# A four-layer kernel: the last layer's polar network cut into 64 pieces and dealt out between the waves of its attention

## The chip, the cores and the metric

The kernel runs on one core of a Trainium2 chip. The core has five engines with a queue of instructions each: TensorE (PE; matrix products, written to the eight banks of PSUM), VectorE (DVE), ScalarE (ACT; functions, from tables that are loaded in sets), GpSimd (POOL) and SyncE (SP, which here only issues transfers). Each engine takes its instructions in order; an instruction waits on semaphores for what others make. The metric is the device time of one execution in microseconds (us). Three runs of the kernel before took 4312.2, 4317.82 and 4314.3 us: a median of 4314.3 us.

## The reference, cut to what matters

The input x has 2 batches of 2048 tokens of width 256. Each of four layers normalises x and adds an attention-like part and a feed-forward part to it. The first three layers (gated linear attention and a mixture of experts; a state-space block and product-key experts; an exponential average with a dense block and a network of binary weights) are the same before and after. The change lies in layer 3:

```python
def _L3_attn_ref(x, q_proj_weight, k_proj_weight, v_proj_weight, o_proj_weight):
    # 16 heads of 16
    q, k, v = (split_heads(x @ w.T) for w in (q_proj_weight, k_proj_weight, v_proj_weight))
    scores = jnp.einsum('bhtc,bhkc->bhtk', q, k) * 16 ** (-0.5)
    scores = jnp.where(causal, scores, -jnp.inf)
    attn = jax.nn.softmax(scores, axis=-1)
    out = jnp.einsum('bhtk,bhkc->bhtc', attn, v)
    return merge_heads(out) @ o_proj_weight.T

def _L3_ffn_ref(x, theta, phi, theta_noise, phi_noise):
    real = jnp.einsum('bti,io->bto', x, jnp.cos(theta + theta_noise))
    imag = jnp.einsum('bti,io->bto', x, jnp.sin(phi + phi_noise))
    return jnp.sqrt(real * real + imag * imag)

xn = _layernorm(x, axis=-1)
x = x + _L3_attn_ref(xn, ...) + _L3_ffn_ref(xn, ...)
```

The second function is called the polar layer here. All arithmetic is in 32-bit floats.

## The kernel before

x stays in SBUF as 32 tiles of 128 tokens by 256 (`g.x`), 16 per batch. Its normalised transpose, `g.xT`, has two blocks of 128 features by 4096 tokens.

**Layer 2's end.** `layer2` runs eight blocks of 512 tokens. The binary network of one block goes beside the dense block of the next, and so the last block's binary network runs alone: PE makes products, ACT and DVE split each into two parts (lines 1009 and 1010, tile `hb`), DVE adds the sum to x (line 1043).

**The polar layer of batch 0.** `four_layers` then opens a pool and calls `layer3_ffn`. It makes the 256 by 512 matrix of cosines and sines, `cs`, in `polar_weights`: eleven DVE operations bring the angles into range, and two ACT operations take the sine. Four times it normalises four tiles (`norm`, line 71), transposes them on PE (`turn`, line 87), multiplies each tile with `cs` (512 columns, two halves of the contraction), squares, sums, takes the root and adds to x. These instructions are placed by the scheduler of the framework.

**The attention.** All of `layer3_attn` from line 1479 on is inside `tc.manual_schedule()`: there the order of each engine's instructions is the order in which the code writes them. Its work goes by eight groups of four heads (two batches by four groups). For a group, `qk` makes queries and keys in eight pieces of 256 tokens: two ACT copies out of PSUM, and four transfers by SP that bring each head's 16 key rows to a partition that is a multiple of 32 (line 1192). `waves` walks over 40 units of a causal score matrix, of 128 by up to 512, with four heads each:

- for one group (`gm`) the scores with queries on the partitions (tile `ps_m`, line 1365), whose row maxima DVE takes (line 1386); `fold` brings the maxima into the query tile of that group;
- for the group before (`ge`), whose maxima are known, the scores with keys on the partitions (tile `ps_e`, line 1361), whose exponential ACT takes into `pt` (line 1375), POOL masks the diagonal (line 1379), and PE multiplies with the values (line 1416, tile `ps_v`). `divide` divides by the sums, `prod` multiplies with the output weights.

A matrix of 32 rows takes a quarter of PE's rows, so four of these scores run side by side. First there is a stage with maxima alone, for group 0; it is called solo here. Seven stages do `ge` and `gm` together: a unit is then two waves, each with two heads of the one and two heads of the other, in the order e, m, e, m. The last stage has `ge` alone.

Between the waves small pieces of work are dealt out: `fill` (one after a unit in the paired stages, at an even pace in the solo stage), `pieces` on PE that have come due through `later`, and `steps` on other engines. In the paired stages a piece borrows one of the four banks of `ps_m`; the exponent scores have three banks. In the solo stage the fill is batch 1's polar layer (`polar`, line 1427: norms on ACT and DVE, transposes, 16 products), the 16 value projections of batch 0 and the eight `qk` pieces of group 1. The values lie in `vals`, 256 columns per token tile; `spread` (line 1209) copies a group's 64 columns on POOL into one of two tiles `vv`, 32 columns per head with a one in the 17th, so that the sum of the probabilities comes out as a 17th row. The value projections of batch 1 are due during the stage of groups 2 and 3.

Of the kernel before, what the change touches and what calls it, by code (L numbers as in the profile page):

```python
# [14 lines left out]
F32 = mybir.dt.float32  # L15
# [1034 lines left out]
def polar_weights(g, pool, a, cs):  # L1050


    nc = g.nc
    th = pool.tile([P, 4, 512], F32, name="th")
    nc.sync.dma_start(th, a["l3_th"])
    an = pool.tile([P, 2, 512], F32, name="an")
    n = pool.tile([P, 2, 512], F32, name="an_n")
    nc.vector.tensor_tensor(an[:, 0, :], th[:, 0, :], th[:, 1, :], ALU.add)
    nc.vector.tensor_tensor(an[:, 1, :], th[:, 2, :], th[:, 3, :], ALU.add)
    nc.vector.tensor_scalar(n[:, 0, :], an[:, 0, :], 0.15915494309189535, 0.25, ALU.mult, ALU.add)  # L1060
    nc.vector.tensor_scalar(n[:, 1, :], an[:, 1, :], 0.15915494309189535, None, ALU.mult)
    nc.vector.tensor_scalar(n, n, 12582912.0, None, ALU.add)
    nc.vector.tensor_scalar(n, n, 12582912.0, None, ALU.subtract)
    for c in (6.28125, 0.0019350051879882812, 3.019916050561733e-07):
        nc.vector.scalar_tensor_tensor(an, n, -c, an, ALU.mult, ALU.add)
    nc.vector.tensor_scalar(an[:, 0, :], an[:, 0, :], 1.5707963267948966, None, ALU.add)
    nc.vector.tensor_scalar(an, an, 3.1415925, -3.1415925, ALU.min, ALU.max)
    for w in range(2):
        nc.scalar.activation(cs[:, :, w * D : (w + 1) * D], an[:, w, :].rearrange("p (k n) -> p k n", k=2), AF.Sin)


def layer3_ffn(g, tc, a):

    nc = g.nc
    F = g.polar
    wk = F.wk
    F.tiny = wk.tile([P, 1], F32, name="tiny", bufs=1)
    nc.vector.memset(F.tiny, TINY)
    F.cs = wk.tile([P, 2, 512], F32, name="cs", bufs=1)
    with tc.tile_pool(name="l3w", bufs=1, side="right") as pw:  # L1080
        polar_weights(g, pw, a, F.cs)
    for n in range(NT // 8):
        xb = g.x[:, 4 * n : 4 * n + 4, :]
        xn = wk.tile([P, 4, D], F32, name="xn3", tag="xn3")
        norm(g, wk, xb, xn, 4)
        turn(g, xn, g.xT[:, :, n * 512 : (n + 1) * 512], 4)
        r = wk.tile([P, 4, D], F32, name="r3", tag="r3")
        for i in range(4):
            t = 4 * n + i
            ps = g.psum()  # L1090
            mm(nc, ps, [(g.xT[:, k, t * P : (t + 1) * P], F.cs[:, k, :]) for k in range(2)])
            sq = wk.tile([P, 2, D], F32, name="sq3", tag="sq3")
            nc.scalar.activation(sq.rearrange("p w d -> p (w d)"), ps, AF.Square)
            nc.vector.scalar_tensor_tensor(r[:, i, :], sq[:, 0, :], TINY, sq[:, 1, :], ALU.max, ALU.add)
        nc.scalar.activation(r, r, AF.Sqrt)
        nc.gpsimd.tensor_tensor(xb, xb, r, ALU.add)

def layer3_attn(g, tc, a, out):
# [15 lines left out]
    with ExitStack() as es:  # L1118
        wk = es.enter_context(tc.tile_pool(name="l3a", bufs=2))
        wb = None  # L1120
        psv = None
        wqk = g.w3a.rearrange("p (k n) -> p k n", k=2)
        wv = g.w3b[:, 0:512].rearrange("p (k n) -> p k n", k=2)
        wo = g.w3b[:, 512:1024].rearrange("p (h n) -> p h n", h=2)
# [15 lines left out]
        vvs, mns, rrs = [], [], []  # L1140
        for i in range(2):
            vv = wk.tile([P, NQ, P], F32, name=f"vv3_{i}", bufs=1)
            nc.gpsimd.memset(vv, 0.0)
# [65 lines left out]
        def spread(G, q):  # L1209
# [6 lines left out]
            if G.n == 3:  # L1216
                for f in v1[4 * q : 4 * q + 4]:
                    later(1, f, True)
# [458 lines left out]
```

## Time and profile before

| stage of the profiled execution | from - to, us | length, us |
|---|---|---|
| layers 0 to 2 | 0 - 2946.8 | 2946.8 |
| polar layer of batch 0 and first projections | 2946.8 - 3017.7 | 70.9 |
| solo: maxima of group 0, with fill | 3017.7 - 3138.3 | 120.6 |
| seven paired stages | 3138.3 - 4203 | 1065 |
| probabilities of group 7 and output | 4203 - 4318.2 | 115 |
| span; time of this execution; median of the runs | | 4318.2; 4319.87; 4314.3 |

Over the span PE is busy 3903.7 us (90%), DVE 2546.8 (59%), ACT 1962.8 (45%) and POOL 1278.5 (30%). A row of the timeline gives the start, the length, the engine, the line of the kernel, the operation, what it writes and reads, and the shape; in brackets stands how long the engine was idle before it and what ended the wait. A group of instructions gives "x count | busy us, mean ns of one | idle us before, and what ended it". A product of 32-bit floats shows as two instructions, one for each pass. PE's weight loads are the engine PEld.

### The profile page before, as it was taken

The numbers are of one execution on the slowest core, as the hardware profiler recorded it, in microseconds if no ns is written. First come the engines' busy times: TensorE is split into PE (matmuls) and PEld (weight loads), VectorE is DVE, ScalarE is ACT, GpSimd is POOL, SyncE is SP. The second block draws the span as 40 slices with busy tenths as digits, with TensorE's granted clock in tenths as the row PEclk, the third lists the DMA queues.
The fourth block names the chain that finished last, engine by engine and source line by source line (L and its number), as shares of the span: only waits on it lengthen the run. The fifth ranks groups of instructions, "written<-read, shape, count | busy, mean of one in ns | idle before, by whom it ended". The sixth has DMA issues, their size and how long they took to land.

```text
span 4318.2 us, 58674 instructions
## 1 busy us (share of the span) xinstructions
PE 3903.7 (90%) x21388; PEld 2310.3 (54%) x21388; DVE 2546.8 (59%) x6485; ACT 1962.8 (45%) x3777; POOL 1278.5 (30%) x1302
## 2 busy tenths in 40 slices
PE   6478988999879999999959999997999999999998
PEld 5356666766745556655636767774433333333332
DVE  6354444454468999999973333234756666666660
ACT  3144333433345555555513232222455555555556
POOL 1502222222256766666652111111211111111101
PEclk8687999999989999999979999998999999999999
DMA  4200122221245667666670000000000000000000
GB/s 177 94 32 32 64 80 80 80 80 64 100 145 163 211 205 220 209 208 214 215 246 1 1 1 1 1 1 24 4 9 7 5 4 17 16 10 9 4 2 26
DMA packets 110802, 330.22 MB, mean 76 GB/s; under 512 B 30609, under 2 KB 63010, under 8 KB 104114
## 3 DMA queue, kind: packets, MB, share of 16 engines
q0 software_dynamic: 52720, 264.15, 19.1%
q1 hardware_dynamic: 55330, 59.41, 4.2%
q8 instruction: 169, 2.77, 0.3%
q10 hardware_dynamic: 2464, 2.91, 0.2%
q14 instruction: 119, 0.97, 0.1%
HBM read 286.56 MB, written 33.03 MB: 74 GB/s over the span
## 4 chain that ended last, share of the span: by engine, by line
PE 53%; DVE 9%; DMA 3%; issue 2%; POOL 2%; ACT 1%; SPq 1%; ACTq 0%; DVEq 0%; POOLq 0%
PE ps_e L1361 12%; PE ps_v L1416 7%; PE ps_a L68 6%; PE ps_f L68 6%; PE ps_c L68 4%; PE ps_m L68 3%; PE ps_k L68 3%; PE ps_m L1365 2%; DMA G<-in_tab_in,ind 2%; DVE hid L817 2%; PE ps_o L1019 1%; PE ps_h L839 1%; PE ps_m L1369 1%; PE ps_x L68 1%; DVE scr L834 1%
## 5 line engine op out<-in xcount | busy, mean ns | idle before, releaser
L1386 DVE TENSOR_REDUCE mp<-ps_m 128x1 f32<-128x512 f32 (+3 forms) x1120 | 629.6, 606 | 393.4 <-PE ps_m L1365 230.3
L1375 ACT ACTIVATE pt<-ps_e 128x512 f32<-128x512 f32 (+3 forms) x1120 | 537.6, 532 | 423.2 <-PE ps_m L1365 284.5
L1365 PE MATMUL ps_m<-kT,qT 32*128 32x512 f32 (+3 forms) x2240 | 665.0, 573 | 0.0
L1361 PE MATMUL ps_e<-qT,kT 32*128 32x512 f32 (+3 forms) x2240 | 659.7, 574 | 3.9 <-ACT qT L1190 3.9
L1361 PEld LDWEIGHTS ps_e<-qT,kT 32*128 32x128 f32 x2240 | 223.9, 183 | 336.8 <-PE ps_m L1365 124.8
L1379 POOL TENSOR_SCALAR_AFFINE_SELECT pt<-pt 128x256 f32<-128x256 f32 x256 | 103.7, 407 | 845.2 <-ACT pt L1375 845.0
L805 POOL DMA_INDIRECT G<-in_tab_in,ind x256 | 274.3, 1071 | 211.3 <-DVE ind L792 64.2
L1416 PE MATMUL ps_v<-pt,vv 128*32 128x512 f32 (+3 forms) x2560 | 313.2, 541 | 1.6 <-POOL pt L1379 0.9
L805 POOL DMA_INDIRECT G<-in_tab_out,ind x256 | 270.3, 1056 | 85.0 <-issue 31.7
L68 PE MATMUL ps_e<-xgT,we 128*128 128x256 f32 x936 | 242.0, 405 | 27.0 <-ACT xgT L306 17.2
L68 PE MATMUL ps_f<-hb,l_b 128*128 128x512 f32 x1024 | 258.8, 405 | 0.0
L68 PE MATMUL ps_k<-wk,xt 128*128 128x512 f32 x512 | 254.2, 607 | 3.0 <-DVE ix L782 2.7
L1365 PEld LDWEIGHTS ps_m<-kT,qT 32*128 32x128 f32 x2240 | 228.9, 183 | 45.7 <-issue 41.0
L1009 ACT ACTIVATE hb<-ps_f 128x512 fp32r<-128x512 f32 x128 | 75.6, 597 | 314.9 <-PE ps_f L68 314.9
L68 PEld LDWEIGHTS ps_f<-hb,l_b 128*128 128x128 f32 x1024 | 190.5, 189 | 48.4 <-issue 6.7
L68 PEld LDWEIGHTS ps_e<-xgT,we 128*128 128x128 f32 x936 | 177.5, 198 | 70.6 <-ACT xgT L306 22.8
L834 DVE CUSTOM_DVE_ANT_0 scr<-hid,G,gate 128x512 f32<-128x512 f32 x256 | 200.4, 783 | 18.2 <-DMA G<-in_tab_out,ind 12.7
L1010 DVE SCALAR_TENSOR_TENSOR hb<-ps_f,hb 128x512 fp32r<-128x512 f32 x128 | 86.6, 684 | 209.2 <-ACT hb L1009 209.1
L494 DVE COPY_PREDICATED AT<-lm,ps_g 128x256 f32<-128x256 uint8 x224 | 104.7, 520 | 142.7 <-PE ps_g L489 142.6
L489 PE MATMUL ps_g<-qt,E 64*128 64x64 f32 x1792 | 138.5, 295 | 33.0 <-DVE E L485 24.2
L817 DVE SCALAR_TENSOR_TENSOR hid<-G,lin,hid 128x512 f32<-128x512 f32 x224 | 166.9, 745 | 2.0
L815 DVE CUSTOM_DVE_ANT_0 scr<-xn,G,gate 128x256 f32<-128x256 f32 x256 | 147.9, 578 | 33.9 <-DMA G<-in_tab_in,ind 33.4
(410 smaller groups left out, 7586.7 us busy)
## 6 DMA issues: line engine op xcount, KB each, us to landing
xgd<-zero SPq DMA_DIRECT2D x13, 768.0 KB, 12.4
xg<-xgd SPq DMA_DIRECT2D x39, 256.0 KB, 2.8
yd<-ye SPq DMA_DIRECT2D x39, 256.0 KB, 3.0
G<-in_tab_in,ind POOLq DMA_INDIRECT x256, 5.0
G<-in_tab_out,ind POOLq DMA_INDIRECT x256, 5.5
kT<-qk SPq DMA_DIRECT2D x256, 16.0 KB, 1.8
out<-x SPq DMA_DIRECT2D x8, 512.0 KB, 3.0
x<-in_x ACTq DMA_DIRECT2D x4, 512.0 KB, 9.5
```

What stands on the lines that cost most here:

```text
L68: nc.tensor.matmul(out, lhsT, rhs, start=(i == 0), stop=(i == n - 1))
L489: nc.tensor.matmul(two[r][:, n * 64 : (n + 1) * 64], E[r * 64 : (r + 1) * 64, n * P : (n + 1) * P], qt[r * 64 : (r + 1) * 64, n * 64 : (n ...
L494: nc.vector.copy_predicated(AT[:, r].rearrange("p e (n t m) -> p e n t m", t=2, m=m)[:, :, :, 1, :], lm[:, li * 64 : (li + 1) * 64].unsque ...
L805: nc.gpsimd.indirect_dma_start(G, None, a[tab], bass.IndirectOffsetOnAxis(ap=k.ind[:, h, j : j + 1], axis=0))
L815: nc.vector.tensor_tensor_reduce(scr[:, 0:D], k.xn[:, j, :], G[:, 0:D], k.gate[:, h, j : j + 1], 0.0, ALU.mult, ALU.add, lin[:, h : h + 1])
L817: nc.vector.scalar_tensor_tensor(hs, G[:, D:768], lin[:, h : h + 1], hid if h == 0 else hs, ALU.mult, ALU.add)
L834: nc.vector.tensor_tensor_reduce(scr, hs, G[:, 0:512], k.gate[:, h, j : j + 1], 0.0, ALU.mult, ALU.add, lout[:, h : h + 1])
L1361: nc.tensor.matmul(te[i // step][:, i % step, c0:512], ge.kT[row(j), kt * P : (kt + 1) * P], ge.qT[row(j), qb * 512 + c0 : (qb + 1) * 512] ...
L1365: nc.tensor.matmul(tm[i // step][:, i % step, 0:w], gm.qT[row(j), qi * P : (qi + 1) * P], gm.kT[row(j), ch * 512 : ch * 512 + w], start=Tr ...
L1375: nc.scalar.activation(pt[:, o : o + step, c0:512], te[i // step][:, :, c0:512], AF.Exp, scale=0.25)
L1386: nc.vector.tensor_reduce(gm.mp[:, qi, j : j + step, ch], tm[i // step][:, :, 0:w], AX.X, ALU.max, negate=True)
L1416: nc.tensor.matmul(av[row(j), c0:512], ge.vv[:, kt, row(j)], pts[j][:, c0:512], start=first, stop=last)
```

## The change

- `layer3_ffn` is gone, and with it the stage between layer 2 and the attention. `polar_weights` works on POOL with tiles it is given, and is called first inside the manual order; a pool on the right side of SBUF whose tiles each wait for the earlier tiles in their place alone holds the angles and the norms.
- Batch 0 is normalised by quarters: quarter 0 as before, the statistics of the other twelve tiles by DVE at once, and the normalisation of each by ACT. Only two of group 0's eight `qk` pieces run before the waves; the other six, with the other quarters' norms and transposes, lead the solo stage's fill. Batch 1's norms and transposes stay in that fill; its polar products leave it.
- The polar layer is 64 pieces: for each of 32 tiles one of 256 columns for the cosines and one for the sines. ACT squares each out of PSUM, POOL sums; after eight tiles one root over 2048 columns on ACT, then four additions to x on POOL. The pieces are dealt out as fill in the first seven paired stages: 11, 11, 10 for batch 0, then 8 in each of four stages.
- One tile `vals` of 288 columns per token tile holds all 16 heads, 17 columns each with the one in place. The product with the probabilities reads 32 columns from a multiple of 17; `spread` and the two `vv` are gone. The value projections of batch 1 come due one by one as group 3's last units have read the old ones, one stage later than before.
- A wave of a paired stage goes e, m, m, e.

```diff
-def polar_weights(g, pool, a, cs):
+def polar_weights(g, a, th, an, n, cs):
...
-    nc.vector.tensor_tensor(an[:, 0, :], th[:, 0, :], th[:, 1, :], ALU.add)
+    nc.gpsimd.tensor_tensor(an[:, 0, :], th[:, 0, :], th[:, 1, :], ALU.add)
...
     for c in (6.28125, 0.0019350051879882812, 3.019916050561733e-07):
-        nc.vector.scalar_tensor_tensor(an, n, -c, an, ALU.mult, ALU.add)
+        nc.gpsimd.tensor_scalar(th[:, 0:2, :], n, -c, None, ALU.mult)
+        nc.gpsimd.tensor_tensor(an, an, th[:, 0:2, :], ALU.add)
...
-def layer3_ffn(g, tc, a):
...
+        wf = esf.enter_context(tc.tile_pool(name="l3f", bufs=2, side="right", reuse_waits="tile"))
...
+        vals = wk.tile([P, NQ, 288], F32, name="vals", bufs=1)
+        vh = vals[:, :, 0:272].rearrange("p t (h e) -> p t h e", e=17)
...
-                    for i in range(len(he)):
-                        if ge:
...
+                    for f, i in ([(e_score, 0), (m_score, 0), (m_score, 1), (e_score, 1)] if both
+                                 else [(e_score if ge else m_score, i) for i in range(4)]):
+                        f(i)
...
-                            nc.tensor.matmul(av[row(j), c0:512], ge.vv[:, kt, row(j)], pts[j][:, c0:512],
+                            nc.tensor.matmul(av[row(j), c0:512], vals[:, kt, at + 17 * j : at + 17 * j + 32], pts[j][:, c0:512],
                                              start=first, stop=last)
+                        if ge.n == 3 and qb == 3:
+                            later(0, v1[kt], True)
...
+        def polar(t8):
+            st = {}
+            def part(i, w):
+                t = 8 * t8 + i
+                ps = f_tile()[:, 0:D]
+                mm(nc, ps, [(g.xT[:, k, t * P : (t + 1) * P], cs[:, k, w * D : (w + 1) * D]) for k in range(2)])
+                if w == 0:
+                    if i == 0:
+                        st["r"] = wk.tile([P, 8, D], F32, name="r3", tag="r3", bufs=1)
+                    nc.scalar.activation(st["r"][:, i, :], ps, AF.Square)
+                    return
+                sq = wk.tile([P, D], F32, name="sq3", tag="sq3")
+                nc.scalar.activation(sq, ps, AF.Square)
+                nc.gpsimd.tensor_tensor(st["r"][:, i, :], st["r"][:, i, :], sq, ALU.add)
+                if i == 7:
+                    later(2, root, False)
+                    for n in range(4):
+                        later(3 + n, lambda n=n: add(n), False)
+            def root():
+                nc.scalar.activation(st["r"], st["r"], AF.Sqrt, bias=tiny)
+            def add(n):
+                ts = slice(8 * t8 + 2 * n, 8 * t8 + 2 * n + 2)
+                nc.gpsimd.tensor_tensor(g.x[:, ts, :], g.x[:, ts, :], st["r"][:, 2 * n : 2 * n + 2, :], ALU.add)
+            return [lambda i=i, w=w: part(i, w) for i in range(8) for w in range(2)]
...
         with tc.manual_schedule():
+            polar_weights(g, a, th, an, an_n, cs)
...
+            norm(g, wf, g.x[:, 0:4, :], xns[0], 4)
...
+            for t in range(12):
+                nc.vector.bn_stats(st[:, t, :], g.x[:, 4 + t, :])
+                nc.vector.bn_aggr(mv[:, t, :], st[:, t, :])
+            for c in range(2):
+                turned(0, 0, c, xns[0])()
+            nc.scalar.activation(rs, mv[:, :, 1], AF.Sqrt, bias=g.eps)
+            for f in qk0[0:2]:
+                f()
...
+            quarter(1)
+            fill = [turned(0, 1, 0, xns[1]), turned(0, 1, 1, xns[1]), *qk0[2:4], lambda: quarter(2),
+                    turned(0, 2, 0, xns[2]), turned(0, 2, 1, xns[2]), *qk0[4:6], lambda: quarter(3),
+                    turned(0, 3, 0, xns[3]), turned(0, 3, 1, xns[3]), *qk0[6:8]]
...
+                b = n8 // 3 if n8 < 6 else 1
+                few = rest[b][: (len(rest[b]) + (3 if not b else 7) - n8 - 1) // ((3 if not b else 7) - n8)] if n8 < 7 else []
+                rest[b] = rest[b][len(few) :]
+                fill = [f for n in range(max(len(fill), len(few))) for f in few[n : n + 1] + fill[n : n + 1]]
                 waves(gs[n8], gs[n8 + 1] if n8 < 7 else None, fill, *tiles)
```

## The prediction

> **Which views, in which order.** The times come first: the profiled execution took 4319.87 us (span 4318.2 us and 1.7 us around it), 5.6 us over the median of the three runs, 4314.3 us. The sum below is made against 4319.87; its difference then goes on the median. Next the busy time by stretch, for what bounds each stage of layer 3; then the timeline at the stages' edges and inside single units; last the groups, for durations.
>
> The stretches, in the columns start:end, length, busy us (instructions) of PE, PE's weight loads, DVE, ACT, POOL, then granted clock, DMA share, GB/s. They are, in order: the polar layer of batch 0; the first projections; the stage in which group 0 has maxima alone ("solo"); two of the seven paired stages; the last group's probabilities.
>
> ```profile
> 2945.00:3001.00 56.00, 37.48 (x101) 17.60 (x99) 39.70 (x87) 19.23 (x31) 19.07 (x15) 0.82 0.11 38
> 3001.00:3017.00 16.00, 10.61 (x31) 7.07 (x32) 0.43 (x1) 5.51 (x14) 2.35 (x1) 0.79 0.08 21
> 3017.00:3138.00 121.00, 111.37 (x590) 52.53 (x589) 85.94 (x94) 55.95 (x148) 22.60 (x25) 0.97 0.02 6
> 3290.00:3442.00 152.00, 152.00 (x1108) 55.08 (x1104) 95.79 (x176) 87.87 (x186) 22.31 (x43) 1.00 0.04 8
> 3442.00:3599.00 157.00, 157.00 (x1158) 58.90 (x1156) 95.95 (x176) 91.21 (x198) 17.09 (x39) 1.00 0.03 6
> 4203.00:4298.00 95.00, 92.92 (x682) 28.57 (x678) 4.89 (x11) 72.43 (x91) 20.32 (x38) 1.00 0.07 20
> ```
>
> See three things. For 72 us no engine is the bound: a chain of hand-overs is, at a clock near 0.8. In the solo stage PE is busy 92%, DVE 71%. In the paired stages PE reads 100%, but overlapped row groups hide waits there, so single units must be read. Here the timeline of one unit with no extra piece of work:
>
> ```profile
> 3371.84 1.07 PE L1416 MATMUL ps_v<-pt,vv 128*32 128x512 f32 x8
> 3372.83 0.69 PE L1361 MATMUL ps_e<-qT,kT 32*128 32x512 f32 x1
> 3374.70 0.18 PEld L1361 LDWEIGHTS ps_e<-qT,kT 32*128 32x128 f32 x1 [0.71 <-ACT pt L1375]
> 3374.71 0.69 PE L1365 MATMUL ps_m<-kT,qT 32*128 32x512 f32 x1
> 3375.76 1.06 PE L1416 MATMUL ps_v<-pt,vv 128*32 128x512 f32 x8
> ```
>
> and units with a piece after the first wave (a value projection, four matmuls of 256 columns):
>
> ```profile
> 3477.83 1.06 PE L1416 MATMUL ps_v<-pt,vv 128*32 128x512 f32 x8
> 3479.90 1.13 PE L68 MATMUL ps_m<-w3b,xT 128*128 128x256 f32 x4
> 3482.03 1.07 PE L1416 MATMUL ps_v<-pt,vv 128*32 128x512 f32 x8
> ```
>
> The first unit takes 3375.76 - 3371.84 = 3.92 us: its second exponent score waits for ACT to free a bank, and the maximum score queued behind it waits too. The other takes 3482.03 - 3477.83 = 4.20 us. A piece of 1.06 us thus costs 0.28 us: the rest fills that wait. In narrow diagonal units a piece costs more (2.65 against 3.21 us, 0.56). Over a stage: the one with 34 pieces runs 157 us, one with 18 runs 151: some 0.36 us a piece. **Paired stages pay 0.36 us for work that costs over a microsecond elsewhere.**
>
> **Part 1, the way into the attention.** Before: layer 2's last x update ends at 2946.8, the first score starts at 3017.7, so 70.9 us. The change takes 16 products of 512 columns, their squares and sums, three of four normalisations and six of eight projections out of it. What stays:
> - Sin twice 1.15, a table load 1.28, the root 0.30: 2949.5, if the angles are ready (below).
> - Four normalisations on DVE. In before such four beside POOL's copies and memsets took 4.99 us, undisturbed 0.40 each. POOL's kT copies (5.6 us) are still there: 5.2 with the reciprocal, to 2954.7.
> - Eight transposes and two copies (0.59 each), to about 2957, beside twelve more statistics on DVE, 12 x 0.56 = 6.7, to 2961.4. ACT's second root waits for these, and behind it in ACT's queue the copies of projections 0 and 1: 2961.7.
> - Those projections feed eight DMAs. SP issues one per 0.587 us, landing takes 1.8: first copy 2962.1, last issue over at 2966.8, landed 2968.6.
>
> So the first score starts at 2968.6: **-49 us**. The hand-overs:
>
> ```profile
> 2961.01 1.15 ACT L1069 ACTIVATE cs<-an 128x512 f32<-128x512 f32 x2 [2.69 <-DVE an L1067]
> 2968.04 4.99 DVE L83 TENSOR_SCALAR xn<-x,ln_mv,ln_rs 128x256 f32<-128x256 f32 x4
> L1192 SPq DMA_DIRECT2D kT<-qk x63: 507/587/1496, 3003.1 to 3139.9; - x63
> ```
>
> The angles move from DVE to POOL, and Sin stands first in ACT's hand-written order: if they are late, every root, copy and projection behind it is. POOL's price by its rows (a two-input operation 1.28 us for 512 columns and 2.35 for 1024; one-input, no such row, 0.93 per 1024 from the kT copy of 2048 in 1.89, or 1.63 from the mask's 0.41 per 256): 17 to 22 us, I take 17, the plain copy being the nearer. The new pool waits tile by tile. By the sizes in the code its two 8 KB tiles lie where layer 2 keeps xs_1 and f2, last read at 2907.7 and 2898.3 in the trace. Their DMA (0.33 us on SP, idle then, 4.9 to land) can be in at 2913, and POOL does under 5 us in the last 67 us of layer 2. So the chain ends near 2932, hidden: cost nothing. Without that cover POOL starts after the kT copies and small memsets, 2946.8 + 8.8, and Sin waits until 2973. Of these 26 us the statistics and the undisturbed normalisations give 6 back: +20.
>
> **Part 2, solo.** PE loses 16 products of four 512-column matmuls 0.43 apart, and 16 changes into that form, 0.2 each (a piece of four 256-column ones takes 1.06, not 4 x 0.21): 30.5 of its 111. It gains six transpose sets (0.6) and six projections (1.06), 10: 91. DVE stays at 88 with batch 1's norms. At before's 92% this is 99; the quarters then hand over three times through ACT (4 x 0.59 us, transposes and projections in line behind), some 2.3 each, 7: 106 us. Bounds: 95 (DVE) and 121. **-15.** The 24 DMAs of the six projections (14 us of SP) run beside it; SP is needed there only for group 1, at the end.
>
> **Part 3, 64 pieces in the paired stages.** Each is four matmuls of 256 columns like a projection: 64 x 0.36 = **+23**. Its Square (0.37 us as L1189's copy) fits: a unit has 4 x 0.60 of exps in 4.2 us. With them 207 of 280 units have a piece, 137 free before, 73 now. Group 3 gets 46 for 40 units, since the second values move there from group 2; the rest spills into group 4, no price. POOL's sums, 32 x 0.72 and 16 x 1.28 us, are 43 us in 1065 and replace 13 of value copies; masks queued behind one have about a unit's slack. I add +3.
>
> **Part 4, the order in a wave.** The maximum score no longer stands behind the exponent score that waits for ACT. That one then runs alone, its two passes 0.42 apart instead of 0.53: 0.2 us in each free unit, some 62 full ones: **-13**. Lower bound 0: it exists only where the wait does.
>
> **Part 5, four roots among the exps.**
>
> ```profile
> L540 ACT ACT_TABLE_LOAD x16 | 20.5, 1283 | 0.3
> L538 ACT ACTIVATE sq<-o 128x128 f32<-128x128 f32 x128 | 37.8, 306 | 0.0
> L1471 ACT ACTIVATE r<-r,tiny 128x1024 f32<-128x1024 f32 x4 | 4.6, 1148 | 3.3 <-POOL r L1469 3.3
> ```
>
> Squares after exps load no table in layer 0 (L538), so the pieces don't; a root does, and the exp after it again: 2 x 1.28 + 2.0 (1024 columns in 1.15, doubled) = 4.6 us of closed ACT. The Trainium skill ("ScalarE: Activation LUTs", What ACT_TABLE_LOAD costs) speaks louder against it: a switch is a 1283 ns load plus about 1380 ns of draining, 2.66 us. Eight switches are 10.3 us by the row, 21.3 by the page; the row's 0.3 us of idle before 16 loads shows no such drain, so I use the row. PE has a piece and most of two waves in hand, so about 3 of 4.6 us come through: 4 x 3 = **+12** (0 to 18; 29 by the page). Behind a root in ACT's queue stand the exps, and PE's values wait for those. The sums have one tile r: the second eight's first Square comes some two units after the first root and may wait for four sums of 1.28 us; 3 us once, left to the range.
>
> **Part 6, values in one tile.** Weight loads keep 32 columns; a start at multiples of 17 is shown by no row: 0, at worst 0.05 us in each of 320 units, 16. The 32 POOL copies go; they waited for nobody long.
>
> **Sum:** -49 - 15 + 23 + 3 - 13 + 12 = -39 us: 4280.9 for a profiled execution, **4275 us** on the median.
>
> **Rivals.**
> - *The angles come late* (POOL's own order puts the kT copies first): +20, 4295. For it: the copies stand earlier in the code. Against: in before POOL runs L1341's memset, written later, ahead of L1096's sum. 18%.
> - *No gain from order and solo*: the waits were others': +13 +8, 4296. 12%.
> - *Solo falls to DVE's 95 us, roots hide*: -11 -8, 4256. 7%.
> - *Slower: a piece costs its whole self.* If its Square stands ahead of the exps PE waits for, a piece costs 1.06 + 0.37 = 1.43, not 0.36: +68, 4343. It decides from 0.36 + 39/64 = 0.97 us a piece. Against it the 34-piece stage; for it ACT, at 60%, gains 24 us of squares and the roots. 17%, some of it near no change.
>
> My own case has 46%, 4262 to 4288 alone. A difference under 0.2% (8.6 us) can't be told from none. All but the last case are faster; of the last, 5 in 17 end within 0.2%. Range 4250 to 4318: it leaves out the best few and the worst dozen in a hundred.
>
> **What would show it.** First score near 2969; Sin just after 2947 with POOL's chain ended before; solo about 106 us; filled units at 4.20 and free ones at 3.7; four table loads to roots and four back, each with a PE gap of about 3 us. Wrong if: POOL's angle work lies after 2947, or filled units go past 4.4 us.

## The result, and the profile after

The changed kernel takes 4349.5 us (median of four runs, 4342.67 to 4351.86) against 4316.06 for the kernel before in the same comparison: a ratio of 1.0075, with a 95% interval of 1.0057 to 1.0092. It is slower by 0.75%; the forecast was 4275.

The profiled execution took 4351.86 us (span 4350.1), 32.0 more than that of before. The marks are those of the front table: layer 2's last x update, the first score (solo begins), the first exponent score (paired stages begin), the first score of the last stage (4204.2 before, 1.2 us later than that table has it).

| stage | before, us | after, us | difference | forecast |
|---|---|---|---|---|
| layers 0 to 2, same code | 2946.8 | 2951.7 | +4.9 | 0 |
| way into the attention | 70.9 | 53.9 | -17.0 | -49 |
| solo | 120.6 | 117.5 | -3.1 | -15 |
| seven paired stages | 1065.9 | 1113.2 | +47.3 | +25 |
| last stage | 113.9 | 113.9 | 0.0 | 0 |

The first row is no effect of the change: in the kernels with the same layers 0 to 2 that ran below on like chips, their end fell anywhere from 2939.0 to 2952.4 us (with the changed kernel ten profiles, mean 2946.8). Layer 3 is therefore compared by its stages; it became 27.1 us longer where 39 less were forecast.

The busy time by stretch, columns as in the prediction: the way in, solo, and groups 1, 2, 3 and 4 of the paired stages.

```profile
2951.70:3005.50 53.80, 5.68 (x16) 3.84 (x16) 13.46 (x41) 7.46 (x16) 36.57 (x25) 0.55 0.10 40
3005.50:3123.00 117.50, 103.58 (x572) 54.44 (x572) 83.28 (x94) 53.52 (x151) 0.00 (x0) 0.91 0.03 8
3277.00:3437.00 160.00, 158.17 (x1153) 59.33 (x1150) 95.89 (x178) 96.47 (x202) 30.20 (x49) 1.00 0.04 7
3437.00:3598.00 161.00, 158.15 (x1128) 57.98 (x1128) 94.60 (x176) 92.87 (x195) 24.19 (x44) 0.98 0.03 6
3598.00:3757.00 159.00, 159.00 (x1176) 61.23 (x1172) 96.70 (x178) 93.58 (x204) 23.80 (x43) 1.00 0.06 17
3757.00:3922.00 165.00, 160.25 (x1150) 60.61 (x1148) 95.48 (x176) 95.38 (x201) 23.64 (x43) 0.97 0.04 9
```

In the first row PE works 5.7 of 53.8 us and POOL 36.6: POOL is the engine that the way in waits for, as the timeline below shows. In groups 1, 2 and 4 PE no longer reads 100%, and in groups 2 and 4 the granted clock falls below 1: these are stages with a root. Group 3, which has none, reads 100% at full clock in spite of its 46 pieces.

The timeline of the way in, cut to the transfers, POOL, ACT and what waits behind ACT:

```profile
2950.46 0.33 SPq L1092 DMA_DIRECT2D w3a<-in_l_wqk  x1
2950.84 0.42 SPq L1094 DMA_DIRECT2D w3b<-in_l_wvo  x1
2951.31 0.42 SPq L1099 DMA_DIRECT2D th<-in_l_th  x1
2951.89 5.56 POOL L1113 COPY kT<-cst 128x2048 f32<-128x2048 f32 x3 [37.64 <-DVE x L1043]
...
2959.95 1.26 POOL L1054 TENSOR_TENSOR an<-th 128x512 f32<-128x512 f32 x1
...
2964.80 2.78 POOL L1058 TENSOR_SCALAR an<-an 128x1024 f32<-128x1024 f32 x1
...
2983.93 2.34 POOL L1062 TENSOR_TENSOR an<-an,th 128x1024 f32<-128x1024 f32 x1
...
2989.00 1.15 ACT L1066 ACTIVATE cs<-an 128x512 f32<-128x512 f32 x2 [37.26 <-POOL an L1064]
2990.16 1.28 ACT L80 ACT_TABLE_LOAD   x1
2991.46 0.30 ACT L80 ACTIVATE ln_rs<-ln_mv,eps 128x4 f32<-128x4 f32 x1
2991.79 0.18 DVE L81 RECIPROCAL ln_rs<-ln_rs 128x4 f32<-128x4 f32 x1 [34.42 <-ACT ln_rs L80]
2992.56 2.21 PE L1446 MATMUL ps_x<-cst,xq 128*128 128x128 f32 x8 [42.18 <-DVE xq L83]
...
3005.54 3.44 PE L1336 MATMUL ps_s<-kT,qT 32*128 32x512 f32 x8 [7.29 <-DMA kT<-qk]
```

POOL idles 37.64 us until layer 2 ends, copies kT, clears small tiles, and only at 2959.95 begins on the angles. SP is late as well: the transfer of the angles, th, stands behind those of two weights, is issued at 2951.31 and lands 6.4 us later, at 2957.7. The angles take until 2989.0, 29 us; an operation with one input and one constant takes 2.78 for 1024 columns, more than one with two inputs (2.34). ACT stands 37.26 us before the sine, and behind the sine stand the first norm's root, DVE and PE.

A paired unit without a piece, to be held against the 3.92 us of before:

```profile
3560.41 1.06 PE L1394 MATMUL ps_v<-pt,vals 128*32 128x512 f32 x8
3561.41 0.69 PE L1331 MATMUL ps_e<-qT,kT 32*128 32x512 f32 x1
...
3563.27 1.12 PE L1331 MATMUL ps_e<-qT,kT 32*128 32x512 f32 x2
3564.32 1.06 PE L1394 MATMUL ps_v<-pt,vals 128*32 128x512 f32 x8
```

It takes 3.91 us. The lone exponent score still takes 1.12 for its two passes, 0.53 apart, not the 0.42 of the forecast. A filled unit takes 4.20, as before (3880.88 to 3885.08).

Last, the second root (group 2): its timeline, and the stretches around it.

```profile
3544.87 1.28 ACT L1433 ACT_TABLE_LOAD   x1
...
3545.79 0.43 PE L1394 MATMUL ps_v<-pt,vals 128*32 128x128 f32 x8
...
3546.17 2.00 ACT L1433 ACTIVATE r<-r,tiny 128x2048 f32<-128x2048 f32 x1
...
3548.18 1.28 ACT L1351 ACT_TABLE_LOAD   x1
...
3550.13 1.32 PE L1331 MATMUL ps_e<-qT,kT 32*128 32x512 f32 x2 [2.85 <-ACT pt L1351]
...
3554.42 1.06 PE L1331 MATMUL ps_e<-qT,kT 32*128 32x512 f32 x1
...
3555.40 1.94 PE L1394 MATMUL ps_v<-pt,vals 128*32 128x512 f32 x8
...
3558.03 0.59 PE L1331 MATMUL ps_e<-qT,kT 32*128 32x512 f32 x1
```

```profile
3545.80:3549.80 4.00, 1.48 (x15) 0.45 (x14) 2.46 (x4) 3.96 (x4) 1.55 (x2) 1.00 0.00 0
3549.80:3553.80 4.00, 3.67 (x8) 1.21 (x12) 0.24 (x1) 1.85 (x4) 3.63 (x4) 0.64 0.00 0
3553.80:3557.80 4.00, 4.00 (x20) 0.82 (x20) 1.74 (x3) 1.09 (x2) 0.00 (x0) 0.51 0.00 0
3557.80:3561.80 4.00, 4.00 (x28) 1.16 (x24) 2.48 (x4) 2.17 (x4) 0.00 (x0) 1.00 0.00 0
```

ACT is closed for 4.6 us and PE stands 2.85 of them, the gap of the forecast. But then the granted clock falls: it reads 0.64 and 0.51 over four us each, and 0.50 throughout from 3551.0 to 3557.7, some seven us. In this time a score of 512 columns takes 1.06 instead of 0.59. Counted from one product with the values to the next, two units take 9.61 and 5.01 us (3545.79 to 3555.40 to 3560.41).

### The profile page after: what moved, and what is told of

Same layout as the page of the kernel before. It is cut to its first block, busy times and chain, and to the rows that moved or that the text cites. A ratio compares the mean times of both kernels' runs of the same rounds, so it can differ in the third digit from the quotient of the medians.

```text
span 4350.1 us, 58832 instructions
## 1 busy us (share of the span) xinstructions
PE 3898.2 (90%) x21516; PEld 2323.5 (53%) x21516; DVE 2515.2 (58%) x6441; ACT 1983.1 (46%) x3827; POOL 1305.7 (30%) x1306
## 4 chain that ended last, share of the span: by engine, by line
PE 52%; DVE 9%; DMA 3%; POOL 2%; issue 2%; ACT 2%; SPq 0%; ACTq 0%; DVEq 0%; POOLq 0%
PE ps_e L1331 12%; PE ps_v L1394 7%; PE ps_a L68 6%; PE ps_f L68 6%; PE ps_c L68 4%; PE ps_m L68 4%; PE ps_k L68 3%; PE ps_m L1336 2%; DMA G<-in_tab_in,ind 2%; DVE hid L817 2%; PE ps_h L839 1%; PE ps_o L1019 1%; PE ps_m L1345 1%; PE ps_s L1331 1%; DVE scr L834 1%
## 5 line engine op out<-in xcount | busy, mean ns | idle before, releaser
L1331 PE MATMUL ps_e<-qT,kT 32*128 32x512 f32 (+3 forms) x2240 | 640.3, 580 | 14.3 <-ACT pt L1351 10.4
L1336 PE MATMUL ps_m<-kT,qT 32*128 32x512 f32 (+3 forms) x2240 | 558.6, 577 | 0.0
L1394 PE MATMUL ps_v<-pt,vals 128*32 128x512 f32 (+3 forms) x2560 | 312.8, 544 | 1.5 <-POOL pt L1355 0.9
L805 POOL DMA_INDIRECT G<-in_tab_out,ind x256 | 271.7, 1061 | 85.0 <-issue 33.1
L834 DVE CUSTOM_DVE_ANT_0 scr<-hid,G,gate 128x512 f32<-128x512 f32 x256 | 199.5, 779 | 16.2 <-DMA G<-in_tab_out,ind 11.0
L1336 PEld LDWEIGHTS ps_m<-kT,qT 32*128 32x128 f32 x2240 | 182.4, 185 | 26.5 <-issue 25.1
```

The source lines that it names most:

```text
L805: nc.gpsimd.indirect_dma_start(G, None, a[tab], bass.IndirectOffsetOnAxis(ap=k.ind[:, h, j : j + 1], axis=0))
L834: nc.vector.tensor_tensor_reduce(scr, hs, G[:, 0:512], k.gate[:, h, j : j + 1], 0.0, ALU.mult, ALU.add, lout[:, h : h + 1])
L1331: nc.tensor.matmul(te[i // step][:, i % step, c0:512], ge.kT[row(j), kt * P : (kt + 1) * P], ge.qT[row(j), qb * 512 + c0 : (qb + 1) * 512] ...
L1336: nc.tensor.matmul(tm[i // step][:, i % step, 0:w], gm.qT[row(j), qi * P : (qi + 1) * P], gm.kT[row(j), ch * 512 : ch * 512 + w], start=Tr ...
L1394: nc.tensor.matmul(av[row(j), c0:512], vals[:, kt, at + 17 * j : at + 17 * j + 32], pts[j][:, c0:512], start=first, stop=last)
```

## The experiments

Theory A: the missing gain lies in three places, and the rest is as costed: the angles, late on POOL, stand in front of the way in (some 33 us); the four roots cost 22 instead of 12, since PE comes out of each gap with a slow clock; the wave order gives nothing. Solo is a fourth, of open cause at this point. The rivals are named in each expectation. All times are medians, with the ratio to the kernel before on the same chip; the stages come from each kernel's own profile. The changed kernel has 53.9, 117.5 and 1113.2 us for way in, solo and paired stages.

| kernel | time, us | ratio (95%) | way in | solo | paired |
|---|---|---|---|---|---|
| sines_later | 4324.84 | 1.0015 (1.0007 to 1.0023) | 21.0 | 122.5 | 1117.3 |
| no_roots | 4326.65 | 1.0021 (1.0014 to 1.0028) | 54.5 | 117.8 | 1091.0 |
| old_order | 4347.41 | 1.0076 (1.0056 to 1.0096) | 53.7 | 117.3 | 1115.5 |
| no_pieces | 4302.19 | 0.9964 (0.9956 to 0.9973) | 53.8 | 117.5 | 1068.4 |
| angles_first | 4345.79 | 1.0050 (1.0034 to 1.0066) | 50.2 | 118.0 | 1113.3 |
| angles_under | 4440.81 | 1.0004 (0.9985 to 1.0022) | 20.8 | 118.2 | 1118.7 |
| warm_roots | 4345.04 | 1.0054 (1.0037 to 1.0071) | 53.6 | 117.9 | 1112.2 |
| warm_half | 4339.45 | 1.0037 (1.0023 to 1.0051) | 53.6 | 118.0 | 1105.3 |
| sines_split | 4303.32 | 0.9959 (0.9940 to 0.9978) | 21.5 | 121.4 | 1098.0 |
| spread_fill | 4294.73 | 0.9934 (0.9915 to 0.9953) | 17.6 | 113.0 | 1094.6 |
| best_a | 4408.67 | 0.9934 (0.9918 to 0.9949) | 16.7 | 110.0 | 1094.3 |
| best_b | 4402.65 | 0.9916 (0.9897 to 0.9936) | 16.2 | 106.7 | 1093.8 |

Three of them (angles_under, best_a, best_b) ran on a chip on which layers 0 to 2 took over 100 us longer, and the kernel before took 4438.19 us; only their ratios and their stages of layer 3 are used.

**The sines moved away.**

```diff
         with tc.manual_schedule():
-            polar_weights(g, a, th, an, an_n, cs)
...
-            fill = [turned(0, 1, 0, xns[1]), ...
+            fill = [lambda: polar_weights(g, a, th, an, an_n, cs), turned(0, 1, 0, xns[1]), ...
...
-                    ..., *qk0[6:8]]
+                    ..., *qk0[6:8], lambda: polar_sines(g, an, cs)]
```

> The changed kernel with the angles' POOL work put after the first stage's memset of maxima and the two sines put on ACT behind the last quarter's normalisation; nothing else is moved. Theory A (ACT stood still for POOL's angles, 37.26 us before the sine): the first score comes 18 to 24 us after layer 2's last x update instead of 53.8, and the time falls by about 30 us, from 4349.5 to about 4319. Rival B (something else holds the first score, for instance the twelve statistics or the transfers, or the solo stage gives the gain back): the first score later than 40 us after layer 2, or the solo stage longer by 15 us and more, so that less than 12 us come off.

The first score comes 21.0 us after layer 2: the chain of hand-overs behind the sine is what the forecast worked out (21.8), and nothing else holds it. The time falls by 24.7 us. Of the 32.9 us of the way in, 5.0 go to a longer solo stage, and the paired stages read 4.1 more, 1.6 of it by slow clock at the first root (shown below). Theory A holds; its 30 was a little high.

**Where the chain could have been.** The forecast said that the angles' tiles are free early, so the chain would lie under layer 2's tail. In angles_first the transfer of th goes ahead of the two weight transfers, and the angle work ahead of the kT copies; in angles_under it goes ahead of the small memsets also (the lines with mn and mns below, and the like for vals and rr).

```diff
+        th = wf.tile([P, 4, 512], F32, name="th", tag="xn")
+        nc.sync.dma_start(th, a["l3_th"])
...
         w3a = w3.tile([P, 1024], F32, name="w3a")
         nc.sync.dma_start(w3a, a["l3_wqk"])
...
-            nc.gpsimd.tensor_copy(kt, one16.to_broadcast([P, S]))
...
-            nc.gpsimd.memset(mn, 0.0)
...
             polar_weights(g, a, th, an, an_n, cs)
+            for kt in kTs:
+                nc.gpsimd.tensor_copy(kt, one16.to_broadcast([P, S]))
+            for mn in mns:
+                nc.gpsimd.memset(mn, 0.0)
```

> The changed kernel with the transfer of the angles ahead of the two weight transfers on SP, and POOL's angle work ahead of the key tiles' copies and the memsets; the sines stay first on ACT. It tests the forecast's claim that the chain can lie under layer 2's end because its tiles are free there. Theory A (the tiles are free, only the order of the queues made the angles late): the transfer is issued before layer 2's last x update, the chain is over by then or a few us after it, and the first score comes 20 to 26 us after layer 2 instead of 53.8: about 4320. Rival B (the tiles wait for layer 2's end whatever the order): the transfer goes at layer 2's end, the chain of 29 us starts some 2 to 3 us later, Sin 32 us after layer 2, first score at about +48: about 4343.

> The changed kernel as in angles_first, and with POOL's small memsets behind the angle chain too, so that nothing that waits for layer 2's end stands ahead of it on POOL. Theory A (the tiles are free near 2913 us, as the run angles_first showed by its transfer; POOL's order alone kept the chain behind): the chain runs under layer 2's tail and ends before layer 2 does, Sin follows layer 2's last work at once, the first score comes 20 to 23 us after layer 2, about 4319. Rival B (one of POOL's angle operations waits for something that ends with layer 2): first score later than +40, over 4335.

The timeline of angles_first:

```profile
2913.31 0.33 SPq L1091 DMA_DIRECT2D th<-in_l_th  x1
...
2952.58 1.13 POOL L1125 MEMSET mn<- 128x512 f32 x2 [37.63 <-DVE x L1043]
2953.65 0.31 POOL L1127 MEMSET vals<- 128x256 f32 x1
...
2955.29 1.26 POOL L1054 TENSOR_TENSOR an<-th 128x512 f32<-128x512 f32 x1
```

The transfer goes at 2913.31. That is 39.1 us before layer 2 ends (2952.4 in this run), as the forecast read it from the kernel before (last read at 2907.7, end at 2946.8). But memsets of tiles that layer 2 still holds stand ahead on POOL, and the way in only falls to 50.2. In size this is rival B's outcome (about 48), but not for its reason: the rows show the tiles free and POOL's order in the way. With the memsets moved as well (angles_under; its layer 2 ends at 3067.6):

```profile
3033.70 1.29 POOL L1054 TENSOR_TENSOR an<-th 128x512 f32<-128x512 f32 x1 [3.47 <-DMA th<-in_l_th]
...
3061.94 1.04 POOL L1064 TENSOR_SCALAR an<-an 128x1024 f32<-128x1024 f32 x1
...
3067.72 1.15 ACT L1066 ACTIVATE cs<-an 128x512 f32<-128x512 f32 x2
```

All of POOL's 29 us lie under layer 2, the sine follows layer 2 at once, and the way in is 20.8 us. So it was the order of the queues alone: what stood ahead of the chain, on POOL and on SP, waited for layer 2. Each of the two would have been enough: with th landing at 2957.7, as in the changed kernel, POOL's chain could have begun at most 2.2 us earlier than it did. No run put only one of them right.

**Without roots, without pieces, and with the old order.**

```diff
-                    later(2, root, False)
```

```diff
-            rest = [[f for t in range(2) for f in polar(2 * b + t)] for b in range(2)]
+            rest = [[], []]
```

```diff
-                    for f, i in ([(e_score, 0), (m_score, 0), (m_score, 1), (e_score, 1)] if both
+                    for f, i in ([(e_score, 0), (m_score, 0), (e_score, 1), (m_score, 1)] if both
```

> The changed kernel without the four roots: the sums of squares are added to x as they are, so one ACT operation over 2048 columns and two table loads go four times. Theory A (each root closes ACT, PE stands about 2.9 us and then runs at half its clock for some 8 us): about 25 us less, 4325, and the units at these places take 4.2 us. Rival B (the long units come from the four additions of 1.28 us each on POOL, before which the masks queue, or from group ends): these units stay at 6 to 10 us and less than 8 us come off.

> The changed kernel without the polar layer's 64 pieces, their squares, sums, roots and additions to x: the second term of the last layer is left out. Theory A (a piece costs 0.36 us beside the waves, and the four roots 25 us): 23 + 25 = 48 us less, about 4301. Rival B (a piece costs its whole self, 1.43 us): 92 + 25, about 4233. Rival C (pieces are hidden wholly): only the roots' 25 us come off, about 4325.

> The changed kernel with its waves in the order e, m, e, m of the kernel before; nothing else is undone. Theory A (the order buys nothing: a free unit takes 3.91 us after and 3.92 before): within 5 us of 4349.5. Rival B (the forecast's step: 0.2 us in each of some 62 free units): 13 us more, about 4362. Rival C (the new order does harm by putting m ahead): 10 us and more less.

Without roots the paired stages fall by 22.2 us to 1091.0; the units that took 9.61 and 5.01 take 3.73 and 3.91. POOL's additions are still there, so they are not the cause. Without pieces as well they fall by another 22.6 to 1068.4: 22.6 / 64 = 0.353 us a piece, against 0.36 forecast. What is left against before is 2.5 us, for the values in one tile, the wave order and the later value projections together. The old order gives 1115.5 against 1113.2 and a ratio of 1.0076 against 1.0075: no effect. Theory A holds in all three.

**Is it the clock or ACT's backlog?** Products that nobody reads, behind each root:

```diff
             def root():
                 nc.scalar.activation(st["r"], st["r"], AF.Sqrt, bias=tiny)
+                ps = f_tile()
+                mm(nc, ps, [(g.ident, cs[:, n % 2, :]) for n in range(6)])
```

> The changed kernel with six extra products of 512 columns on PE (about 2.6 us, their result is read by nobody) behind each of the four roots, so that PE works while ACT is closed. Theory A (a root costs 6 to 7 us in three of four places because PE stands 2.9 us and then runs some 8 us at half its clock): PE's gap shrinks to under 1.5 us, no passes at half speed follow, and the four roots together cost 10 to 14 us instead of 22, so about 10 us less than 4349.5 in spite of 10.4 us of added products. Rival B (the cost is ACT's backlog of exps, the clock only goes along with it): the products add to it or change nothing, 0 to 10 us more.

> As warm_roots, with three extra products behind each root instead of six: six took 5.4 us there, not the 2.6 that its expectation counted, so three take 2.7 and just fill PE's gap of 2.9 us. Theory A (a root costs PE's gap and, in three of four places, some 4 us of half-speed work after it): the gap falls under 1 us, the half-speed stretch goes, the units at the four roots cost 10 to 13 us more than without roots instead of 23, and the seven paired stages take about 1102 us instead of 1113. Rival B (ACT's backlog sets the price, the clock only goes along): the four roots cost 22 us and more, the paired stages 1113 to 1124.

Six products took 5.4 us, twice what the expectation counted. So 21.6 us of work were added, and the paired stages did not grow (1112.2): the gap and the slow passes were gone. But the products cost what the roots had cost, so the saving of 10 us that theory A expected did not come, and in time alone the run ends as rival B said. Three products (2.8 us), just the gap, tell the two apart. The stretches around the same root in warm_half:

```profile
3544.00:3548.00 4.00, 4.00 (x24) 1.52 (x24) 0.49 (x2) 3.80 (x5) 0.43 (x3) 1.00 0.00 0
3548.00:3552.00 4.00, 3.54 (x21) 1.00 (x22) 2.58 (x4) 3.38 (x5) 4.00 (x4) 1.00 0.00 0
3552.00:3556.00 4.00, 4.00 (x32) 1.26 (x31) 2.73 (x5) 1.82 (x4) 1.18 (x2) 1.00 0.00 0
```

PE stands 0.46 us instead of 2.85, and the clock stays at 1.00. Unit by unit against no_roots the four roots now cost 2.95 + 3.78 + 3.13 + 3.77 = 13.6 us; in the changed kernel they cost 2.94 + 6.98 + 6.92 + 6.39 = 23.2. Theory A had 10 to 13, rival B 22 and more. The paired stages, 1105.3, lie 3 us over theory A's 1102 and 8 under the rival's 1113. ACT is closed for as long as before, so about 10 of the 23 us are the slow clock. The first root of the four bears it out: there PE's gap was 1.83 us, no slow stretch followed, and it cost 2.94.

It is not the length of the gap alone that decides. In sines_later the first root has the same gap, and the clock falls:

```profile
3308.35 1.12 PE L1334 MATMUL ps_e<-qT,kT 32*128 32x512 f32 x2 [1.83 <-ACT pt L1354]
```

```profile
3306.50:3309.80 3.30, 1.47 (x7) 0.67 (x5) 1.29 (x2) 3.06 (x5) 3.30 (x3) 1.00 0.09 20
3310.00:3313.30 3.30, 3.30 (x15) 1.01 (x17) 0.21 (x1) 1.10 (x4) 1.39 (x2) 0.50 0.03 6
```

Here the half clock lasts 3.4 us and the root costs 4.5; in angles_under, again with a gap of 1.83, it lasts 6.8 us and the root costs 6.2. This is one part of why the paired stages of kernels that differ only ahead of them read up to 5.5 us apart. What decides between these cases no run settles.

**Roots without table switches.**

```diff
+def table(nc, n):
+    nc.scalar.add_instruction(mybir.InstLoadActFuncSet(name=nc.get_next_instruction_name(), act_func_set_id=n))
...
+            table(nc, 6)
             v1 = values(1)
...
-                nc.scalar.activation(st["r"], st["r"], AF.Sqrt, bias=tiny)
+                r = st["r"][:, 2 * n : 2 * n + 2, :]
+                nc.scalar.activation(r, r, AF.Ln, bias=tiny)
+                nc.scalar.activation(r, r, AF.Exp, scale=0.5)
```

> The changed kernel with the sines and angles moved as in the run sines_later, and each root made as an exponential of half a logarithm, in four steps of 512 columns, from a table set that holds both functions and is loaded once before the paired stages, so that no table is switched there. Theory A (the roots' price is switches and a closed ACT, not the arithmetic): the paired stages fall from about 1115 us to about 1093, as without roots, and the time to about 4303, under the kernel before by 0.3%. Rival B (32 more ACT operations of about 0.6 us between the exps cost what the roots cost): the paired stages stay over 1105, the time near 4320.

The paired stages take 1098.0 us, 15 to 19 under the changed kernel and sines_later, 7 over no_roots. At 4303.32 it is faster than the kernel before, 0.9959. Theory A's direction holds, five us short of its 1093; the 32 operations keep some 7 us.

**Solo.** The stretches of solo in the changed kernel:

```profile
3005.50:3015.30 9.80, 9.76 (x38) 6.29 (x39) 4.18 (x4) 1.27 (x3) 0.00 (x0) 0.51 0.01 3
3015.30:3093.70 78.40, 73.41 (x448) 38.30 (x446) 62.34 (x74) 42.99 (x126) 0.00 (x0) 1.00 0.02 6
3093.70:3103.50 9.80, 6.86 (x26) 2.81 (x24) 5.07 (x7) 3.25 (x6) 0.00 (x0) 0.50 0.00 0
3103.50:3123.00 19.50, 13.55 (x70) 7.04 (x64) 11.69 (x10) 6.01 (x17) 0.00 (x0) 0.94 0.09 22
```

There are three bad stretches: ten us at half clock after the idle way in, ten more at half clock later, and an end in which PE works 13.55 of 19.5 us, because a projection's copy waits until earlier transfers have freed one of the two tiles `qk`:

```profile
3112.09 0.37 ACT L1168 COPY qk<-ps_x 128x256 f32<-128x256 f32 x1 [1.90 <-DMA kT<-qk]
...
3114.51 0.37 ACT L1168 COPY qk<-ps_x 128x256 f32<-128x256 f32 x1 [1.67 <-DMA kT<-qk]
```

The end is not new. The last 20.1 us of solo in the kernel before, which has the same eight projections there:

```profile
3118.20:3138.30 20.10, 14.45 (x75) 7.35 (x73) 11.69 (x10) 7.49 (x20) 4.70 (x7) 0.96 0.09 22
```

So it is a loss that the change kept, and not one that it made; the two stretches at half clock are longer than before's, which has one of 0.86 at the start and one of 0.83 later, each over ten us.

Three kernels change these, the first on top of sines_split and each next on top of the one before (best_a also has the queue order of angles_under; its cut shows only the new lines):

```diff
-            nc.scalar.activation(rs, mv[:, :, 1], AF.Sqrt, bias=g.eps)
             for f in qk0[0:2]:
                 f()
+            nc.scalar.activation(rs, mv[:, :, 1], AF.Sqrt, bias=g.eps)
...
-            v = values(0)
+            v, q1 = values(0), qk(gs[1])
+            v = [f for i in range(8) for f in (*v[2 * i : 2 * i + 2], q1[i])]
...
-            fill += qk(gs[1])
```

> The kernel of sines_split with two things moved around the solo stage: the eight projections of group 1 are dealt out among the value projections instead of all at the end, and on ACT the root over the twelve statistics stands behind the copies of the first two projections. Theory A (the end of solo waits for SP, which issues the 32 transfers of those projections at 0.59 us each, and the entry for the statistics): the first score comes some 17 us after layer 2 instead of 21, solo takes about 110 us instead of 122, and the time is 12 to 16 us under that of sines_split, about 4289. Rival B (solo is held by PE's clock and by DVE's bursts of maxima, the transfers are hidden): solo stays within 4 us of sines_split's.

```diff
+            polar_weights(g, a, th, an, an_n, cs)
...
             norm(g, wf, g.x[:, 0:4, :], xns[0], 4)
+            nc.vector.tensor_copy(idb, g.ident)
+            nc.vector.tensor_copy(mkb, g.cst[:, CST["maskq"] : CST["maskq"] + P])
```

> All changes that paid together: the angle chain under layer 2 as in angles_under, the sines in the solo stage's fill, roots as half logarithms in a common table set, group 1's projections spread in the solo stage, and DVE's two casts of the mask and the identity behind the first quarter's normalisation instead of ahead of its statistics. Theory A (in the run spread_fill the casts, 1.9 us each beside POOL's copies, stand in the chain to the first score): first score 13 to 15 us after layer 2 instead of 17.6, about 3 us under spread_fill, ratio to the kernel before near 0.993. Rival B (the casts move the same wait to the first mask, or the POOL copies slow the statistics instead): first score at +17 and no gain over spread_fill.

```diff
+            mm(nc, f_tile(), [(g.ident, g.cst[:, 0:512]) for n in range(5)])
             nc.scalar.activation(rs, mv[:, :, 1], AF.Sqrt, bias=g.eps)
```

> The kernel of best_a with five extra products of 512 columns on PE after the first two projections, while PE waits for the keys' transfers (their result is read by nobody). Theory A (the first 30 us of solo run at a granted clock of 0.6 to 0.9 because PE comes out of an idle stretch): the first 10 us of solo at a clock over 0.85 and solo 4 to 6 us shorter than best_a's. Rival B (the clock is low there because the work itself is thin, with PE waiting on ACT and transfers between small pieces): the clock falls again after the products and solo stays within 2 us.

In spread_fill solo falls from 121.4 to 113.0 (theory A had 110) and the way in from 21.5 to 17.6: together the 12 us that theory A had at the low end, while the medians differ by 8.6. best_a gains 0.9 of the way in and 3.0 of solo, less than hoped for the casts: the way in stays at 16.7, near rival B's 17, and the ratio is that of spread_fill. In best_b PE comes to the first score warm; the first two stretches of solo of best_a (from 3071.90) and of best_b (from 3098.50):

```profile
3071.90:3081.90 10.00, 9.99 (x40) 6.52 (x40) 4.18 (x4) 1.74 (x5) 0.00 (x0) 0.56 0.02 5
3081.90:3091.90 10.00, 9.12 (x62) 5.06 (x60) 4.53 (x7) 5.51 (x13) 0.00 (x0) 1.00 0.06 15
```

```profile
3098.50:3108.50 10.00, 9.12 (x57) 5.27 (x56) 5.47 (x6) 5.15 (x12) 0.00 (x0) 1.00 0.04 11
3108.50:3118.50 10.00, 9.34 (x65) 5.33 (x66) 5.06 (x7) 5.20 (x11) 0.00 (x0) 1.00 0.07 17
```

The clock is 1.00 instead of 0.56, PE does 57 product instructions in the first stretch instead of 40, and solo is 3.3 us shorter, 106.7, a little under theory A's 4 to 6 and over rival B's 2. So the slow start was the idle way in, not thin work. best_b beats both kernels: 0.9916 of the kernel before, 0.8% faster.

## Why the prediction was wrong

From the forecast of -39 us to the measured +32 there are 71 us: 32 in the way in, 12 in solo, 22 in the paired stages, 5 in layers 0 to 2 that are no effect of the change.

- **Part 1, wrong, the largest term.** The failing step is "So the chain ends near 2932, hidden: cost nothing". Its first half was right: the tiles are free 39 us before layer 2 ends. But it looked only at what the chain itself waits for, not at what stands ahead of it in the order of two engines: on POOL the kT copies and memsets, on SP ("idle then") the transfers of two weights, all for tiles that layer 2 holds. The rival that the angles come late named this mechanism, at 18%; the argument against it, that one memset had run ahead of its place in the code, did not bear on these. A second step failed on top: "I take 17, the plain copy being the nearer". The chain took 29.0 us, over the 17 to 22 of the bounds, since POOL's operations with one input and one constant (lines 1058, 1059, 1061) take 2.77 us for 1024 columns, three times the copy's price of 0.93; only those with two constants (1.04 at line 1064) come near it. So late angles cost 33 us (53.9 - 20.8), not the 20 of the rival. The chain from the sine to the first score was right: 21.8 forecast, 20.8 and 21.0 measured once the angles are out of the way.
- **Part 2, wrong.** "At before's 92% this is 99" kept a share that belonged to a PE that came in working, at 0.80 of its clock. Here it came out of 42.18 us of idleness and a last wait of 7.29, and the first ten us ran at 0.51. And "SP is needed there only for group 1, at the end" names a wait without a price: the last 19.5 us are held up by those transfers, as in the kernel before, so that this part did not shrink with PE's work. The runs give 8.4 us for spreading them (on top of sines_split, whose solo is 3.9 longer) and 3.3 for the warm start; with both, on the best kernel, solo is at 106.7 us, where the forecast had 106. The stretch at half clock from 3093.7 was not tested by itself: in the trace a reciprocal stands behind 13.7 us of maxima in DVE's queue and PE waits 2.89 us for it. But this wait starts at 3094.2, and just before it, from 3093.6, the clock already reads 0.50, so the wait is not its cause; the cause stays open.
- **Part 3, right.** 0.353 us a piece against 0.36. The 3 us added for POOL's queue may be in the 2.5 that no run has split.
- **Part 4, wrong by its 13 us.** The lone exponent score does not run at 0.42 but at 0.53, with no other score beside it, so a free unit takes 3.91. The lower bound was the truth.
- **Part 5, the mechanism right and the size off.** PE's gap is the "about 3 of 4.6 us" of the forecast (1.83 to 2.88). What was left out is the clock after it, which cost some 3 to 4 us at three of the four roots: 22.2 us for the stages instead of 12, over the 18 of the range. The 29 us by the page's switch price lie nearer the truth, but not by their reason: ACT stood 0.2 us in all before the nine loads of these stages, and no draining of 1.38 us is to be seen.
- **Part 6, right**: nothing that can be told apart.
- **The rivals.** The one with no gain from order and solo had the order right and most of solo (-3 of -15). The slower one (a piece costs its whole self, 4343) came near the measured time by luck: a piece cost 0.353 us. The forecast's case for a slower kernel should have been three terms, each under 35 us: at the way in, at the roots and in solo.

The Trainium skill ("TensorE: Matmul & The Clock Gate", Part 1, the HAM clock gate) says that PE's clock is halved after an idle window of about 3.4 us and comes back after a busy one. For the way in the rows agree: PE idles 42.18 us and starts solo at 0.51, which the forecast did not weigh. For the roots they do not: by the page the four gaps of under 3 us would be safe, and the roots would cost 12; by the rows three of the four, of 2.85 to 2.88 us, end at a clock of 0.5 for 6.8, 10.2 and 6.8 us, and in sines_later the gap of 1.83 us does so too. The measurement decides.

## What to carry to other kernels

Work hides under another stage only if everything ahead of it in its engine's queue can run there too, and ahead of its transfer in the issuing engine's queue: read the queues, not only the tiles. A short closure of one engine that starves PE is to be costed with the slow clock that may follow, here as much again as the gap. Filling the gap with PE work kept the clock up and took 7.9 us off the paired stages; doing away with the closure, by steps without a table switch (sines_split), took off 15.2. When a stage loses work, ask what it will wait for then, at its start (a PE at half clock) and at its end (a queue of transfers).

## What the runs showed of the hardware that was not expected

- On POOL an operation with one input and one constant took 2.77 us for 128x1024, one with two inputs 2.34, but one with two constants (minimum and maximum, line 1064) 1.04; for 128x512 the multiply and add of line 1056 took 0.61, the single operations of lines 1057 and 1063 took 1.50. Whether a neutral second constant would quicken the others was not tried.
- In the changed kernel PE gaps of 2.85 to 2.88 us were followed by 6.8, 10.2 and 6.8 us at half clock, and a gap of 1.83 was not; in sines_later and angles_under the gap of 1.83 was, by 3.4 and 6.8 us. With 2.8 us of products at each of the four roots the clock stayed at 1.00 there.
- A score that runs alone on its 32 rows has its two passes of 512 columns 0.53 us apart, with a maximum score beside it (the kernel before) as without.
- A table switch shows as 1.283 us for the load and almost no idle time ahead of it; 32 logarithms and exponentials of 512 columns from one common set cost the paired stages some 7 us against no roots at all, where four roots with eight switches cost 22.
